# Tokens of the first two pairs by two queues, and two warming-up products fewer

## The chip, the cores and the metric

The kernel runs on one core of a Trainium2 chip. A core has a matrix engine (TensorE, PE in the profile; its weight loads are PEld), a vector engine (VectorE, DVE), a scalar engine (ScalarE, ACT), GpSimd (POOL) and a sync engine (SyncE, SP). Transfers between the chip's main memory and the on-chip memory run on 16 DMA engines; here SP and ACT issue them, each into a queue of its own (q1 is SP's, q10 is ACT's in the trace). The metric is the time of one execution on the device in microseconds; lower is better.

## The reference

The input is 16 sequences (B) of 256 tokens (T) of 128 features (C). Twelve layers of attention without softmax follow each other, each with 16 heads of 8 features; then a layer norm of input plus result, a feed-forward block and a second layer norm:

```
x = inputs
for i in range(12):
    q, k, v = split(x @ Wqkv[i].T + bqkv[i])       # heads of 8 features
    att = einsum('bhqd,bhkd->bhqk', q, k) / sqrt(8)
    y = einsum('bhqk,bhkd->bhqd', att, v)
    x = y @ Wproj[i].T + bproj[i] + x
x = layernorm(inputs + x)
g, u = x @ (w_gate/127).T, x @ (w_up/127).T
out = layernorm(x + (silu(g) * u) @ (w_down/127).T)
```

Since there is no softmax, the tokens enter the twelve layers only through their Gram matrix and their mean.

## The kernel before

The 16 sequences are taken as 8 **pairs** (PB = 2 batches each, L32 to L36), and the pairs as two **sets** of four (G = 4). Each pair has 512 tokens, 256 KB. Its tokens are loaded into `xtoks[p]`, a view of the tile `qgv` with four chunks of 128 tokens, each with a column of ones beside it (L220 to L223). Chunks 0 and 1 are the pair's first batch, 2 and 3 its second.

**Start.** VectorE fills `zero` and the columns of ones, and PE makes WARM = 30 products of zeros, which are used nowhere, while the first tokens are on their way (L224, L225). ACT issues the q weights of layer 0 (`wq0s`, L241), warms up its table (L243) and issues the biases (`bcol`, L244).

**Loads.** `load` (L263) hands the planner one operation on SP with a cost of 4 ns a KB. The loop at L268 asks for the tokens of the eight pairs, with prio -9 + 0.01 p. `prep_weights` (L279) asks for each layer's weights; layer 0's have prio -9 too (L282, L283).

**Prologue of a pair** (L326 to L355). `gram` makes four fp32 products on PE (L336, two records each in the trace), one for each chunk of 128 tokens, summed by batch. VectorE takes means from the sums (L340 to L342), PE turns them into rows (L346), ACT or VectorE copies these out (L349, a helper at L205 or L207), and VectorE takes the means' product off the Gram matrix (L353). Then come `products` (L455, the Gram matrix by the value weights), `heads` (L380 and L499, then L509 to L511 on VectorE and GpSimd, then L517), and `projection` (L529 and L530, L534 to L536, L541). From layer 1 on, products L434 to L444 come ahead of them. The q side of layer 0 is a copy of `wq0s` into each pair's `qgv` tile (`first_q`, L469), which must wait until the pair's Gram products have read the tokens there. At the end the feed-forward block goes pair by pair (L706 to L736).

**Who sets the order.** Every operation from the loads on goes through `Plan`. It holds a cost for each engine that could do the operation, and the operations that must come before it. `run` (L118) repeats one step: it finds the earliest start of each operation whose predecessors are placed, and among those that could start first it takes the one with the lowest number

```
(_, end, e), o = min(((b, o) for b, o in found if b[0] <= first), key=lambda x: (x[1].prio - TAILW * x[1].tail, -x[1].tail, x[1].n))
```

with TAILW = 0.0001 (L53, L145). The tail of an operation is its own least cost, plus 300, plus the longest tail of the operations that use its result:

```
o.tail = min(o.costs.values()) + 300 + max((u.tail for u in o.users), default=0)
```

(L124). The engines then carry out their instructions in the order in which the planner placed them, and real waits are semaphores on the data. The planner believes that a load is there 3000 ns after its end on SP (AFTER, at the head of the planner's part). Instructions that are issued outside the planner, such as L241 and L244 on ACT, come ahead in their engine's order; the planner doesn't know of them.

Of the kernel before, what the change touches and what calls it, by code (L numbers as in the profile page):

```python
# [21 lines left out]
C = 128  # L22
# [3 lines left out]
PB = 2  # L26
NP = B // PB
# [7 lines left out]
N = PB * T  # L35
K = N // 128  # L36
G = 4
NO = NP // G
OB = G * PB
WARM = 30  # L40


OSTEP = 0.5
# [148 lines left out]
def linear_attention_ffn_kernel(ctx: ExitStack, tc: tile.TileContext, x, xt, wall, wq0, bias, wg, wu, wd, out):  # L192
    nc = tc.nc
# [27 lines left out]
    xtoks = [t.rearrange("p (k c) -> p k c", c=C + 1) for t in qgvs]  # L221
    for t in xtoks:
        nc.vector.memset(t[:, :, C:], 1.0)  # L223
    for _ in range(WARM):  # L224
        nc.tensor.matmul(banks[7][:, :128], zero, zero, start=True, stop=True)  # L225
# [11 lines left out]
    mhalf = new("mhalf", [K])  # L237
    nc.gpsimd.memset(mhalf, -0.5)

    bcol, wq0s = new("bcol", [L, 4]), new("wq0s", [C])  # L240
    nc.scalar.dma_start(wq0s, wq0)  # L241

# [20 lines left out]
    def load(dst, src, vs, prio, kb=256, reads=[]):  # L263
        plan.op({SP: kb * 4}, lambda e: nc.sync.dma_start(dst, src), reads, vs, prio)


    vq, vgv = [Val() for _ in range(NP)], [Val() for _ in range(NP)]
    for p in range(NP):  # L268
        load(xtoks[p][:, :, 0:C], x[p * N : (p + 1) * N, :].rearrange("(k p) c -> p k c", p=128), [vq[p], vgv[p]], -9 + 0.01 * p)

# [528 lines left out]
```

## Time and profile before

| What | us |
|---|---|
| median of four runs (lowest, highest) | 305.72 (305.21, 306.1) |
| the execution that was profiled | 306.1 |
| its span, first to last instruction | 304.1 |
| PE busy | 294.9 (97%) |
| VectorE busy | 226.6 (75%) |
| ACT busy | 218.0 (72%) |
| GpSimd busy | 138.0 (45%) |
| first warming-up product on PE | 1.04 |
| first Gram product on PE | 4.28 |
| SP's issue of tokens and first weights | 0.79 to 6.29 |
| ACT's issue of q weights, of biases | 0.79, 5.04 |

How to read it: all times within the profile count from the span's first instruction. "Busy" of an engine is the union of its instructions' times. A line such as L336 is a line of the kernel file; where a helper issues an operation, the line is the helper's. The chain of waits is followed back from the last instruction, at each step to what released it. A queue's rows give its packets, megabytes and the share of 16 engines' time. Of a DMA, the profile gives when it was issued and the time from there to its landing.

### The profile page before, as it was taken

To read this page: it belongs to the slowest core of one execution; us is meant where nothing else is said; L and a number is where in the kernel's file an instruction comes from. 1 tells how busy PE (TensorE), PEld (TensorE's weight loads), DVE (VectorE), ACT (ScalarE), POOL (GpSimd) and SP (SyncE) were. 2 spreads that over 40 slices of the span, in tenths; PEclk is the share of its full clock that TensorE was granted. 3 is DMA by queue.
4 is the path that set the end of the run, shared out by engine and by line. 5 is a ranking of instruction groups with operands and counts; after the bars stand their busy time and mean duration, and the time that the engine had idled before them with its cause. 6 is when DMAs were issued, how large, how long until landed. Compare 5 with 4: busy or idle time off the path is not lost.

```text
span 304.1 us, 12834 instructions
## 1 busy us (share of the span) xinstructions
PE 294.9 (97%) x5376; PEld 270.3 (89%) x5376; DVE 226.6 (75%) x683; ACT 218.0 (72%) x559; POOL 138.0 (45%) x208
## 2 busy tenths in 40 slices
PE   8999999999999999999999999999999999999981
PEld 8989999999999999999998999989999998878760
DVE  4796877777677676876767777776654789999993
ACT  3557777767777768777686676776787658778875
POOL 8146452334531445215431354234431157777883
PEclk9999999999999999999999999999999999999999
DMA  7634213112031130311302101220000000000225
GB/s 213 159 95 125 72 39 86 40 42 85 3 88 37 40 88 4 88 41 28 98 2 56 37 11 47 57 63 22 2 2 2 5 1 2 0 0 6 66 70 138
DMA packets 22489, 15.65 MB, mean 51 GB/s; under 512 B 1952, under 2 KB 19872, under 8 KB 22432
## 3 DMA queue, kind: packets, MB, share of 16 engines
q1 hardware_dynamic: 21872, 14.62, 17.7%
q8 instruction: 42, 0.69, 0.9%
q10 hardware_dynamic: 560, 0.22, 0.3%
q14 instruction: 15, 0.12, 0.1%
HBM read 8.02 MB, written 2.10 MB: 33 GB/s over the span
## 4 chain that ended last, share of the span: by engine, by line
PE 87%; DVE 10%; issue 1%; ACT 1%; POOLq 0%; POOL 0%; DVEq 0%
PE bank L455 14%; PE bank L434 8%; PE bank L517 8%; PE bank L436 7%; PE bank L435 7%; PE bank L442 5%; PE bank L499 5%; PE bank L536 4%; PE bank L534 4%; PE bank L535 4%; PE bank L443 3%; PE bank L444 3%; PE bank L336 3%; DVE st L618 2%; PE bank L706 2%; PE bank L707 2%
## 5 line engine op out<-in xcount | busy, mean ns | idle before, releaser
L210 POOL TENSOR_TENSOR thl<-tst,thl 128x260 fp32r<-128x260 f32 x88 | 64.9, 768 | 123.6 <-ACT thl L205 123.6
L205 ACT COPY qgv<-bank 128x256 f32<-128x256 f32 x169 | 59.9, 378 | 19.0 <-PE bank L444 12.8
L205 ACT COPY kv<-bank 128x512 f32<-128x512 f32 (+1 forms) x93 | 53.4, 576 | 19.8 <-PE bank L436 14.4
L434 PE MATMUL bank<-whl,thl 128*128 128x256 f32 x176 | 51.9, 295 | 0.0
L436 PE MATMUL bank<-whl,thl 128*128 128x256 f32 x176 | 49.7, 282 | 0.0
L435 PE MATMUL bank<-whl,thl 128*128 128x256 f32 x176 | 49.4, 281 | 0.0
L455 PE MATMUL bank<-kv,g 128*128 128x128 f32 x352 | 46.1, 275 | 0.0
L541 DVE TENSOR_TENSOR tst<-bank,tst 128x260 f32<-128x260 f32 x96 | 36.9, 424 | 9.7 <-PE bank L536 9.3
L205 ACT CAST thl<-tst 128x260 fp32r<-128x260 f32 x88 | 33.0, 408 | 14.5 <-DVE tst L541 14.4
L455 PEld LDWEIGHTS bank<-kv,g 128*128 128x128 f32 x352 | 42.7, 191 | 0.4 <-issue 0.4
L448 DVE TENSOR_SCALAR qgv<-bank,bcol 128x2 f32<-128x2 f32 x88 | 19.1, 220 | 28.3 <-ACT qgv L205 22.9
L434 PEld LDWEIGHTS bank<-whl,thl 128*128 128x128 f32 x176 | 33.1, 188 | 4.0 <-issue 3.8
L530 DVE TENSOR_TENSOR yhl<-bank,yhl 128x260 fp32r<-128x260 f32 x96 | 34.4, 418 | 2.2 <-ACT yhl L205 2.1
L436 PEld LDWEIGHTS bank<-whl,thl 128*128 128x128 f32 x176 | 33.1, 188 | 0.2 <-POOL thl L210 0.2
L435 PEld LDWEIGHTS bank<-whl,thl 128*128 128x128 f32 x176 | 33.2, 189 | 0.0
L442 PE MATMUL bank<-thl,whl 128*128 128x260 f32 x88 | 28.8, 327 | 0.0
L205 ACT CAST yhl<-bank 128x260 fp32r<-128x260 f32 (+1 forms) x61 | 22.0, 408 | 8.5 <-PE bank L517 7.9
L207 DVE CAST yhl<-bank 128x260 fp32r<-128x260 f32 (+1 forms) x43 | 16.8, 430 | 13.0 <-PE bank L517 13.0
L517 PE MATMUL bank<-qgv,gm 32*32 32x130 f32 x1536 | 26.1, 280 | 0.4 <-issue 0.2
L443 PE MATMUL bank<-thl,whl 128*128 128x260 f32 x88 | 24.8, 282 | 0.0
L444 PE MATMUL bank<-thl,whl 128*128 128x260 f32 x88 | 24.7, 281 | 0.0
L517 PEld LDWEIGHTS bank<-qgv,gm 32*32 32x32 f32 x1536 | 17.3, 103 | 5.9 <-issue 0.5
(157 smaller groups left out, 696.0 us busy)
## 6 DMA issues: line engine op xcount, KB each, us to landing
wraw<-wall SPq DMA_DIRECT2D x12, 256.0 KB, 2.9
wpt<-whl SPq DMA_DIRECT2D x24, 96.0 KB, 2.2
qgv<-x SPq DMA_DIRECT2D x8, 256.0 KB, 5.0
xt<-xt SPq DMA_DIRECT2D x8, 256.0 KB, 3.2
out<-kv SPq DMA_DIRECT2D x7, 256.0 KB, 2.3
wpt<-whl SPq DMA_DIRECT2D x24, 64.0 KB, 2.7
wpt<-whl SPq DMA_DIRECT2D x24, 32.0 KB, 1.9
wraw<-wg SPq DMA_DIRECT2D x1, 192.0 KB, 3.5
```

The lines of the kernel that those rows point to most:

```text
L205: nc.scalar.copy(dst, src)
L210: (nc.vector if e == DVE else nc.gpsimd).tensor_tensor(dst, a, b, ALU.subtract)
L434: nc.tensor.matmul(o, hi[:, b, 0:C], hl(0, 1, 2), start=True, stop=False)
L435: nc.tensor.matmul(o, hi[:, b, 0:C], hl(1, 1, 2), start=False, stop=False)
L436: nc.tensor.matmul(o, lo[:, b, 0:C], hl(0, 1, 2), start=False, stop=True)
L442: nc.tensor.matmul(o, hl(0, 0), flat(hi), start=True, stop=False)
L443: nc.tensor.matmul(o, hl(0, 0), flat(lo), start=False, stop=False)
L444: nc.tensor.matmul(o, hl(1, 0), flat(hi), start=False, stop=True)
L455: nc.tensor.matmul(bank(pgv)[:, b * C : (b + 1) * C], g0[p][:, b, :], tv(b), start=True, stop=True)
L517: nc.tensor.matmul(bank(pys[r])[group(g + r), b * W : (b + 1) * W], gm[group(g), r * PB + b, :], qss[p][group(g), b, :], start=True, stop= ...
L530: plan.op({DVE: dve(PB * W)}, lambda e: nc.vector.tensor_tensor(yl, bank(py)[:, : PB * W], yh.bitcast(F32), ALU.subtract), [py, vyh[p]], [ ...
L541: plan.op({DVE: dve(PB * W)}, lambda e: nc.vector.tensor_tensor(ts, bank(pw)[:, : PB * W], ts, ALU.add), [pw], [vt[p], vc[p]], prio)
```

## The change

The number of warming-up products goes from 30 to 28. The tokens of pairs 0 and 1 (SPLIT = 2) are loaded in two halves: ACT issues the second batch of each, ahead of the q weights and the biases and outside the planner; SP loads the first batch through the planner, with a cost for 128 KB in place of 256 KB. The other six pairs are loaded as before.

```diff
-WARM = 30
+SPLIT = 2
+WARM = 28
...
     nc.gpsimd.memset(mhalf, -0.5)
 
+    half = lambda a, b: a[:, b * (K // PB) : (b + 1) * (K // PB)]
+    tokens = [x[p * N : (p + 1) * N, :].rearrange("(k p) c -> p k c", p=128) for p in range(NP)]
+    for p in range(SPLIT):
+        nc.scalar.dma_start(half(xtoks[p], 1)[:, :, 0:C], half(tokens[p], 1))
+
     bcol, wq0s = new("bcol", [L, 4]), new("wq0s", [C])
     nc.scalar.dma_start(wq0s, wq0)
...
     vq, vgv = [Val() for _ in range(NP)], [Val() for _ in range(NP)]
     for p in range(NP):
-        load(xtoks[p][:, :, 0:C], x[p * N : (p + 1) * N, :].rearrange("(k p) c -> p k c", p=128), [vq[p], vgv[p]], -9 + 0.01 * p)
+        cut = (lambda a: half(a, 0)) if p < SPLIT else (lambda a: a)
+        load(cut(xtoks[p])[:, :, 0:C], cut(tokens[p]), [vq[p], vgv[p]], -9 + 0.01 * p, 256 // (1 + (p < SPLIT)))
```

## The prediction

> **What bounds the kernel now.** I read the page first: TensorE (PE) is busy for nearly the whole span, so what delays PE at the start delays everything behind it.
>
> ```profile
> PE 294.9 (97%) x5376; PEld 270.3 (89%) x5376; DVE 226.6 (75%) x683; ACT 218.0 (72%) x559; POOL 138.0 (45%) x208
> ```
>
> The stretches of the span say the same: PE is busy 60.00 of 60 us from 60 to 120, 59.82 from 120 to 180, 59.83 from 180 to 240 and 39.61 of 40 from 240 to 280. So I take a delay of the first products one to one to the end. The chain of waits from 0.7 to 9 us (start, us, what) is PE alone:
>
> ```profile
> 1.04 3.38 PE bank L225 x30
> 4.42 2.56 PE bank L336 x16
> 6.98 0.22 PE bank L346 x2
> 7.20 0.90 PE bank L336 x8
> 8.10 0.22 PE bank L346 x2
> ```
>
> Thirty warming-up products, then the gram products (L336): eight records a pair, two pairs, then one pair at a time. Eight take 0.90 later, so sixteen should take 1.8; these take 2.56. Two reasons. The weight loads show a small wait for tokens (a gap of 0.10 between the last warming-up load and the first gram load):
>
> ```profile
> 4.00 0.15 PEld L225 LDWEIGHTS <-zero 128*128 128x128 bf16 x1
> 4.25 0.29 PEld L336 LDWEIGHTS bank<-qgv 128*128 128x128 f32 x1
> ```
>
> And up to 5.70 PE goes at half speed: gram products start 0.214 us apart before that point and 0.112 after it (starts of single instructions; the granted-clock column says 1.00 throughout and doesn't show this). In two stretches of 1.40 us each, the gram products and their loads:
>
> ```profile
> 4.30:5.70 1.40, 1.40 (x6) 1.40 (x7) 1.00 1.07 265
> 5.70:7.10 1.40, 1.34 (x12) 1.26 (x12) 1.00 1.01 322
> ```
>
> So a microsecond gained or lost before 5.70 is worth half a microsecond, one after it a whole one.
>
> Next the queues. SP issues four pairs, layer 0's weights, four pairs; ACT issues the q weights at 0.79 and the biases at 5.04:
>
> ```profile
> 0.79 2.08 SPq L264 DMA_DIRECT2D qgv<-x  x4
> 2.92 0.50 SPq L283 DMA_DIRECT2D wraw<-wall  x1
> 3.46 2.83 SPq L264 DMA_DIRECT2D qgv<-x  x4
> ```
>
> The DMA answers for the first four issues, one by one (issue times 0.79, 1.28, 1.82, 2.37; last figure: us from issue to landing):
>
> ```profile
> qgv<-x SPq DMA_DIRECT2D x1, 256.0 KB, 3.4
> qgv<-x SPq DMA_DIRECT2D x1, 256.0 KB, 3.7
> qgv<-x SPq DMA_DIRECT2D x1, 256.0 KB, 4.4
> qgv<-x SPq DMA_DIRECT2D x1, 256.0 KB, 4.8
> ```
>
> They land at 4.2, 5.0, 6.2 and 7.2, about 1.0 us for each 256 KB. PE loads the first pair at 4.25, the second at 5.82, the third at 6.93 and the fourth at 8.04 (single starts): slack 0.8, 0.7 and 0.8, none on the first.
>
> **What the change does to the order.** The diff halves the planner cost of pairs 0 and 1 (from 256 x 4 = 1024 to 512). The planner (L145) takes, of loads that could start at once, the one with the lowest prio - 0.0001 x tail, and the tail holds the load's own cost (L124). Pairs 0 to 3 have the same operations behind them, so the same tail; only prio, -9 + 0.01 p, orders them now. With 512 less tail, pairs 0 and 1 go back by 0.0001 x 512 = 0.0512, which is more than the 0.02 between pair 0 and pair 2. Against a common number: pair 2 at 0.02, pair 3 at 0.03, pair 0 at 0.0512, pair 1 at 0.0612. So **SP issues pair 2, pair 3, then the halves of 0 and 1**, and PE, which the planner puts in order by the same arrival times, starts with gram products of pairs 2 and 3. The weights, now behind the fourth load, lie further back and stay there. The halves that ACT sends at 0.79 belong to pairs wanted third and fourth. (Planner costs are used here for order only, never as times.)
>
> **Part by part.** *Two warming-up products less* (30 start in 1.04 to 4.11, 0.107 apart): PE is free 0.21 earlier, at about 4.0. It waits for tokens in any case: 0. If the tokens were there, 0.21 at half speed would be worth 0.11.
>
> *Pair 2 first, 256 KB by SP, with ACT's 256 KB beside it where 64 KB of q weights lie now.* Packets by queue (q1 is SP, q10 is ACT) from 2.75 to 3.25, then from 3.25 to 3.75:
>
> ```profile
> q1 hardware_dynamic: 248, 0.13, 84.3%
> q10 hardware_dynamic: 91, 0.04, 27.9%
> ...
> q1 hardware_dynamic: 341, 0.17, 112.1%
> ```
>
> 339 packets with two queues, 341 with one: from 2.75 on the queues share one rate. Before that ACT's came on top (SP 91 alone in 1.75 to 2.25; 111 and 48 in 2.25 to 2.75). SP's first pair is 512 packets: 91 + 111 + 248 = 450 by 3.25, the rest 0.09 later. If ACT goes on, SP has between half of 340 per 0.5 us (372 by 3.25, the rest 0.41 later: 0.32 late) and the 73% seen (0.03 late). I take 0.2 late: landing 4.4, first load about 4.45. Ends: 0.2 early (64 KB no longer beside it, at the 332 to 338 GB/s of these rows) and 0.6 late (equal shares throughout: 512 KB are down now at 5.0, less those 64 KB). At half speed 0.2 is worth **+0.1**, the ends -0.1 and +0.3.
>
> The Trainium skill (DMA: Bandwidth & Descriptors, "Issuing engines are not separate DMA queues") speaks against the change: a transfer started on another engine runs on the same 16 DMA engines and saves only issue time. The rows agree from 2.75 us on and disagree before it. By the rule alone pair 2 would share from its first packet, and the sum would be some 0.1 us higher.
>
> *Pair 3 second.* It is whole when SP has moved 512 KB; ACT's 320 KB (two halves, q weights) go beside it, 832 KB in all. Today 832 KB are down when the third pair lands: 3 x 256 + 64, at 6.2. The second gram would be due at 5.82 + 0.1, and a load comes some 0.1 after the landing: 6.3 instead of 5.92, a wait of about 0.35, at full speed; I take **+0.3**, as most of that landing's 16 parts come earlier than its last. Ends: 0 (ACT gives way; 512 KB are down at 5.0) and 0.4.
>
> *Pairs 0 and 1 third and fourth.* At 960 and 1088 KB, so 6.2 to 7.2, and due from 7.3 and 8.4: 0, hidden behind grams of pairs 2 and 3. Weights and pairs 4 to 7 have the same bytes before them as now: 0.
>
> *ACT's queue.* q weights land behind two halves, near 6; their copies (5.55, 6.58, 7.69 on ACT) are first read by L517 at 18.66. Biases go out at 5.04 now, just when the second pair lands, though ACT was done with its warming-up at 3.20; with two more DMAs ahead I expect 5.7 to 6.3. Behind that issue stand the first copies; ACT idles 2.36, 0.61 and 0.71 us before the first three, which covers it. The biases are first read at 15.33. Cost 0; without that cover, the row copies at 8.35 would come late and cost what exceeds 0.3. SP still issues nine DMAs and then idles from 6.3 to 9.49, which hides a later issue: 0.
>
> *The planner behind it.* Weights come one pair's cost earlier in its list, so it may put a gram ahead of an L455, or layer 1's weight cast on ACT. PE's sum of work is the same: 0, but with ends of 0.6 either way, one late or early cast (0.42) and subtraction (0.35) in the stage at 19.67 to 20.78, where the chain runs over VectorE.
>
> **Sum:** 0 + 0.1 + 0.3 = +0.4. The profiled execution took 306.1 (span 304.1, 2.0 around it), so 306.5 by its own terms; it is the slowest of four, whose median is 305.72. On that: **306.1**, +0.13%; the ends of the terms but the planner's (-0.1 to +0.7) make 305.6 to 306.4. About 0.2% (0.61 us) is what a measurement of this kernel can tell from no change.
>
> **Rivals.** *It does what it says*: pair 0 comes first, in halves. For it: the diff's plain text. Against: the 0.0512. SP's half of pair 0 then needs 256 packets instead of 512, landing about 0.5 earlier; PE starts at 4.0 instead of 4.25 at half speed: -0.12, and -0.1 more at most: 305.5.
>
> *The clock opens late (the other side).* Full speed came 4.66 us after the first product (1.04 to 5.70). A hole of 0.1 didn't hinder it; I expect one of 0.3 to 0.5 at 4.0 to 4.5. If a hole of that length makes the count start anew, it opens near 4.45 + 4.66 = 9.1: 3.4 us more at half speed cost 1.7, 307.8. It decides from whatever hole length counts as idle, which no row here shows. Against it: a hole this short is a tenth of the stretch.
>
> *The planner's new order hits a tight stage.* Slower: +0.6 on top, 306.7. Faster: -0.7 on the median if a stage loosens, 305.0 (the middle is full, so only the first 25 us and the last 15 offer anything).
>
> **Chances.** Forecast 0.56, of which 0.10 over 306.33 (both ends late: 0.7); does what it says 0.06 (0.01 of it faster); late clock 0.08; new order slower 0.20, faster 0.10. So faster 0.11, same 0.51, slower 0.38. The range leaves out the late clock and about a tenth more: 305.1 to 306.9.
>
> **What would show it.** Right: the first SP load is waited for by the first gram, with PE idle 0.3 to 0.5 after the 28th warming-up product; SP's row has two issues of 256 KB ahead of two of 128; sixteen gram products end near 7.2 instead of 6.98 with a wait inside; from there the stretches look as before, 0.4 later. Wrong: a first gram at 4.0; 128 KB issues first on SP; half-speed products after 6; or an equal start and a different last 15 us, which would be the planner's order.

## The result

Times in us. "Before" was timed again beside the changed kernel.

| | median | lowest to highest | executions |
|---|---|---|---|
| before | 305.78 | 304.83 to 306.66 | 76 |
| changed | 305.89 | 305.39 to 308.28 | 53 |
| changed, those up to 306.5 | 305.73 (mean 305.79) | 305.39 to 306.5 | 38 |
| changed, those from 307.06 on | mean 307.69 | 307.06 to 308.28 | 15 |

The ratio is 1.0019, 95% interval 1.001 to 1.0028: a loss of 0.6 us in the mean (306.33 against 305.74). The median, 0.11 higher, hides how it comes about. The changed kernel's times form two groups with nothing between 306.5 and 307.06, and before has no execution over 306.66 in these 76. The lower group's mean is 0.05 above before's; nearly all of the loss is the 15 executions of the upper group (15/53 x 1.9 = 0.54).

The execution that was profiled is one of the lower group: 305.59, span 303.9. So its profile shows what the change costs when all goes well, and not the loss.

### The profile page after: what moved, and what is told of

Read it like the earlier page. It is cut to its first block, busy times and chain, and to the rows that moved or that the text cites. A ratio compares the mean times of both kernels' runs of the same rounds, so it can differ in the third digit from the quotient of the medians.

```text
span 303.9 us, 12833 instructions
## 1 busy us (share of the span) xinstructions
PE 294.6 (97%) x5374; PEld 270.0 (89%) x5374; DVE 229.2 (75%) x686; ACT 217.2 (71%) x559; POOL 136.5 (45%) x205
## 4 chain that ended last, share of the span: by engine, by line
PE 86%; DVE 10%; DMA 1%; issue 1%; ACT 1%; POOLq 0%; POOL 0%; DVEq 0%
PE bank L462 14%; PE bank L441 8%; PE bank L524 8%; PE bank L443 7%; PE bank L442 7%; PE bank L449 5%; PE bank L506 5%; PE bank L543 4%; PE bank L541 4%; PE bank L542 4%; PE bank L450 3%; PE bank L451 3%; PE bank L343 3%; DVE st L625 2%; PE bank L713 2%; PE bank L714 2%
## 5 line engine op out<-in xcount | busy, mean ns | idle before, releaser
L206 ACT COPY kv<-bank 128x512 f32<-128x512 f32 (+1 forms) x90 | 51.6, 575 | 19.3 <-PE bank L443 13.5
L524 PE MATMUL bank<-qgv,gm 32*32 32x130 f32 x1536 | 25.9, 280 | 0.2 <-DVE gm L214 0.2
L524 PEld LDWEIGHTS bank<-qgv,gm 32*32 32x32 f32 x1536 | 17.4, 103 | 5.3 <-ACT kv L206 0.4
```

The lines of the kernel that those rows point to most:

```text
L206: nc.scalar.copy(dst, src)
L524: nc.tensor.matmul(bank(pys[r])[group(g + r), b * W : (b + 1) * W], gm[group(g), r * PB + b, :], qss[p][group(g), b, :], start=True, stop= ...
```

## The profile after

The busy times are close to those of before:

```profile
PE 294.6 (97%) x5374; PEld 270.0 (89%) x5374; DVE 229.2 (75%) x686; ACT 217.2 (71%) x559; POOL 136.5 (45%) x205
```

PE's timeline from 0 to 8 us (start, busy, line, operation, number of products; in brackets the idle time ahead and what ended it):

```profile
1.04 3.17 PE L226 MATMUL bank<-zero 128*128 128x128 bf16 x28 [1.04 <-DVE qgv L224]
4.62 2.58 PE L343 MATMUL bank<-qgv 128*128 128x129 f32 x16 [0.41 <-DMA qgv<-x]
7.03 0.38 PE L353 MATMUL bank<-ident,means 128*128 128x128 f32 x2
7.25 1.06 PE L343 MATMUL bank<-qgv 128*128 128x129 f32 x8
```

The 28 warming-up products are over at 4.21, and PE then has nothing to do for 0.41, until the first tokens have landed. No second wait follows: the other 15 gram products and the next pair's come without a bracket. In two stretches cut where the trace records full clock, at 5.78 (before: 5.70), the gram line alone (columns: PE busy with its products, PEld busy with its loads, granted clock, DMA share, GB/s) has 5 products in 1.18 us and 13 in 1.22:

```profile
4.60:5.78 1.18, 1.17 (x5) 1.18 (x6) 1.00 1.22 290
5.78:7.00 1.22, 1.22 (x13) 1.22 (x11) 1.00 1.10 334
```

The granted-clock column says 1.00 in both. The change of pace shows only in the counts.

Which tokens land when, from the DMA answers (size, then us from issue to landing), issue by issue. First SP's, issued at 0.79, 1.29 and 1.82:

```profile
qgv<-x SPq DMA_DIRECT2D x1, 256.0 KB, 3.7
qgv<-x SPq DMA_DIRECT2D x1, 256.0 KB, 4.5
qgv<-x SPq DMA_DIRECT2D x1, 128.0 KB, 4.5
```

Whole pairs come first on SP, and the half of pair 0 third. The first whole pair lands at 4.48 (the chain of waits has 3.69 from 0.79), the second at 5.8, pair 0's half at 6.3. ACT's two halves, both issued by 1.3, land at 4.2 and 5.9. ACT's own timeline:

```profile
0.79 1.05 ACTq L244 DMA_DIRECT2D qgv<-x  x2
1.87 0.52 ACTq L247 DMA_DIRECT2D wq0s<-wq  x1
...
6.29 0.40 ACTq L250 DMA_DIRECT2D bcol<-bias  x1
6.87 0.71 ACT L206 COPY qgv<-wq0s 128x256 f32<-128x256 f32 x2 [2.95 <-PE bank L343]
```

**Where the time went in this execution.** I laid the starts of the 24 groups of 64 small products (L517 before, L524 after) of the two traces side by side. The first comes 0.20 later than before, the second 0.30, and those from the third to the sixteenth, at 162 us, 0.31. Inside the sixteenth, before loses 0.53 that the changed kernel doesn't, and from there on the changed kernel is 0.21 to 0.23 ahead, which is the span's 0.2. That loss at 162 comes and goes by execution (last section); it isn't the change's.

## The experiments

Two theories stood against each other for the upper group. **Late clock**: the hole between the warming-up products and the first gram is sometimes long enough that full clock comes one step later. **Planner's order**: the order of pairs 2, 3, 0, 1 meets a tight stage in some executions. Beside them the sizes of the prediction's terms were to be tested. The median of before stands beside each group of runs, since it differs by chip.

**The order undone, the halves kept** (before 305.82). Only the cost argument goes, so that the planner takes the pairs 0 to 3 in order again:

```diff
-        load(cut(xtoks[p])[:, :, 0:C], cut(tokens[p]), [vq[p], vgv[p]], -9 + 0.01 * p, 256 // (1 + (p < SPLIT)))
+        load(cut(xtoks[p])[:, :, 0:C], cut(tokens[p]), [vq[p], vgv[p]], -9 + 0.01 * p)
```

> The changed kernel with the full planner cost (1024) for all eight loads, so that SP issues the halves of pairs 0 and 1 first and PE keeps the order of before. Theory (the planner's new order makes the hole in front of the first Gram products, and the hole makes the clock open late in about a quarter of the executions): first SP half lands by 3.9, first Gram load at 3.9 to 4.05, no hole over 0.15, no group of times above 307, and a median 0.1 to 0.3 under before (305.78). Rival (two queues at the start are the harm, whatever the order): first Gram load after 4.3, group above 307 stays, median 305.9.

Measured: 306.07 (305.24 to 306.98, 12 executions), ratio 1.0007 (0.9988 to 1.0027), none over 307. SP's first half lands at 3.34, ACT's at 3.59, and the first gram starts at 4.00, with no hole. So the cost argument alone makes the order, and with the pairs in order the upper group isn't seen in 12. The gain of an early start isn't there, though, and PE's timeline shows who takes it:

```profile
4.00 2.15 PE L343 MATMUL bank<-qgv 128*128 128x129 f32 x16
...
6.55 1.16 PE L343 MATMUL bank<-qgv 128*128 128x129 f32 x8 [0.17 <-DMA qgv<-x]
```

The clock opened at 4.31 in this execution, the grams of two pairs were done at 6.2, and the third waited for pair 2, which landed at 6.51. Here the third landing bounds the start, not the first.

**The hole filled** (same chip): the changed kernel with 34 warming-up products.

```diff
-WARM = 28
+WARM = 34
```

> The changed kernel with 34 warming-up products in place of 28, so that PE has no hole while it waits for pair 2; all else as in the changed kernel. Theory (the hole makes the clock open late): no executions above 306.8, the rest as in the changed kernel within 0.1 to 0.2, so a mean of 305.8 to 305.9 and a ratio to before near 1.000. Rival (the late group comes from elsewhere, late landings or a reordered stage): 15 of 53 above 307 as in the changed kernel, ratio near 1.002.

Measured: 305.77 (305.1 to 306.45, 12), ratio 0.9998 (0.9981 to 1.0014). The first pair landed as late as in the changed kernel (4.49), and the first gram starts at 4.64 with no idle time ahead of it:

```profile
4.64 2.71 PE L343 MATMUL bank<-qgv 128*128 128x129 f32 x16
```

The upper group is gone with the hole, and the order is unchanged: this speaks for the late clock.

**A hole in the kernel before** (same chip): 24 warming-up products in place of 30.

```diff
-WARM = 30
+WARM = 24
```

> The kernel before with 24 warming-up products in place of 30; loads, queues and order as before. It makes a hole of some 0.45 (by PE's records) in front of the first Gram products, with no other part of the change. Theory (the hole alone opens the clock late): two groups of times, some 15 to 50 in 100 executions 1.5 to 2.5 above the rest, ratio 1.002 to 1.004. Rival (the hole is harmless, the landings or the order are not): one group, 304.8 to 306.7, ratio 0.999 to 1.001.

Measured: 305.62 (304.95 to 306.79, 12), ratio 0.9998 (0.9977 to 1.0019). A hole of 0.44 is there, the median is before's, and no upper group is set apart:

```profile
4.22 2.26 PE L336 MATMUL bank<-qgv 128*128 128x129 f32 x16 [0.44 <-DMA qgv<-x]
```

So "any hole makes the clock late" fell, and the theory had to say how long the hole must be.

**The order alone**, on two chips (before 305.82 and 305.34): the kernel before with the changed costs, and nothing loaded by ACT.

```diff
-        load(xtoks[p][:, :, 0:C], x[p * N : (p + 1) * N, :].rearrange("(k p) c -> p k c", p=128), [vq[p], vgv[p]], -9 + 0.01 * p)
+        load(xtoks[p][:, :, 0:C], x[p * N : (p + 1) * N, :].rearrange("(k p) c -> p k c", p=128), [vq[p], vgv[p]], -9 + 0.01 * p, 256 // (1 + (p < 2)))
```

> The kernel before with only the planner's cost of pairs 0 and 1 halved: whole pairs by SP in the order 2, 3, 0, 1, all 30 warming-up products, no tokens by ACT. Theory (the order does harm only because ACT's halves share the rate): first Gram load at 4.25 as before, no group above 307, ratio 0.998 to 1.001; the planner's new order downstream shows alone, and the 0.5 that PE loses at 162 us in the trace of before and not in the changed one may go. Rival (the new order costs by itself): ratio above 1.001.

> Once more the kernel before with only the planner's cost of pairs 0 and 1 halved (whole pairs by SP in the order 2, 3, 0, 1; 30 products), for a narrower interval. Theory (the order by itself costs nothing, and takes layer 1's weights to SP's queue at 6.3 in place of 14.3): no late group, median 0.0 to 0.3 under before, ratio 0.998 to 1.000. Rival (the earlier 0.9988 was chance): ratio 1.000 to 1.0015.

Measured: 305.68 (304.86 to 306.33, 12), ratio 0.9988 (0.9971 to 1.0005), and 305.09 (304.5 to 306.34, 12), ratio 0.9992 (0.9977 to 1.0008). None of the 24 is in an upper group, so the order theory fell: no cost of the new order is seen, and the intervals leave room for 0.0008 of the time at most. Both medians are a little under before's (0.14 and 0.25), but neither interval leaves 1 out.

**The changed kernel again** (before 305.89), unedited, for a profile of a late execution.

> The changed kernel itself once more, beside the next three. Theory (its hole of 0.4, longer in some executions when pair 2 lands late, makes the clock open a window later): 2 to 6 of 12 executions between 307.0 and 308.3, none of them with a clock that opened before 8, the rest 305.3 to 306.5. Rival (the late group of the first 53 came from one chip or one session): none above 307, median 305.7 to 305.9.

Measured: 306.0 (305.44 to 307.99, 12), ratio 1.0014 (0.9999 to 1.0029). Two of the twelve are late (307.95, 307.99), and the profiled one is the last of these. Its first pair landed at 4.70. PE's timeline, and the gram line in three stretches (columns as above):

```profile
4.83 3.78 PE L343 MATMUL bank<-qgv 128*128 128x129 f32 x16 [0.62 <-DMA qgv<-x]
8.40 0.64 PE L353 MATMUL bank<-ident,means 128*128 128x128 f32 x2
```

```profile
4.90:6.60 1.70, 1.70 (x8) 1.70 (x9) 1.00 1.19 311
6.70:8.60 1.90, 1.90 (x9) 1.61 (x8) 1.00 1.17 319
8.80:10.20 1.40, 1.37 (x7) 1.40 (x8) 1.00 1.21 292
```

The hole is 0.62 and not 0.41, and half speed lasts until 10.2: eight products in 1.70 us, nine in 1.90, seven in 1.40, always some 0.21 each, where the other execution took 0.1 each from 5.78 on. The sixteen grams take 3.78 in place of 2.58. The trace records full clock from 10.205 on for 293.55 us; in the 305.59 execution from 5.78 on for 296.96. The two lengths differ by 3.41, but a length alone doesn't tell a late opening: in the second profile of the order alone it is 293.55 as well, with an opening at 6.02. The groups of small products, up to the sixteenth, start 2.4 to 2.6 later than before's. This is the prediction's late-clock rival, seen.

**Longer holes in both kernels**: fewer warming-up products in the kernel before (18 beside 305.89, 21 beside 305.34) and in the changed one (22 beside 305.89).

```diff
-WARM = 30
+WARM = 18
```

```diff
-WARM = 28
+WARM = 22
```

```diff
-WARM = 30
+WARM = 21
```

> The kernel before with 18 warming-up products in place of 30: a hole of about 1.1 in front of the first Gram products, with loads, queues and order as before. 24 products made a hole of 0.44 and no late group. Theory (the length of the hole decides): a late group of a quarter to two thirds of the executions, 1.5 to 2.0 above the rest, mean 306.3 to 307.0. Rival (not the hole, but how ACT's halves and the new order spread the arrivals): one group up to 306.9, mean 305.6 to 306.0.

> The changed kernel with 22 warming-up products in place of 28, so that its hole grows from 0.4 to about 1.05. Theory (length of the hole): the late group grows from 28% to over half of the executions, mean above 306.7. Rival (the hole is not it): 28% or none, mean as the changed kernel's, 305.9 to 306.4.

> The kernel before with 21 warming-up products in place of 30: a hole of about 0.7, between the 0.44 of 24 products (none of 12 late) and the 0.8 to 1.1 of 18 (8 of 8 at or above 306.4). Theory (the length of the hole decides, somewhere between 0.41, which passed, and 0.62, which failed): part of the executions late, a quarter to all of those whose window holds the hole, mean 306.1 to 306.8. Rival (no threshold of length): as with 24 products, mean 305.7 to 305.9 and none over 307.

Measured: 306.79 (306.42 to 307.95, 8), ratio 1.0039 (1.0022 to 1.0056); 307.05 (306.4 to 308.07, 6), ratio 1.0046 (1.0029 to 1.0064); and 307.14 (305.17 to 307.55, 12), ratio 1.0053 (1.0036 to 1.007). Full clock comes at 8.50, 9.26 and 9.97. The first gram line of each, in that order:

```profile
3.96 3.78 PE L336 MATMUL bank<-qgv 128*128 128x129 f32 x16 [0.81 <-DMA qgv<-x]
```

```profile
4.71 3.78 PE L343 MATMUL bank<-qgv 128*128 128x129 f32 x16 [1.14 <-DMA qgv<-x]
```

```profile
4.06 3.78 PE L336 MATMUL bank<-qgv 128*128 128x129 f32 x16 [0.60 <-DMA qgv<-x]
```

The 3.78 is the mark of sixteen grams wholly at half speed. The kernel before, in its own order and with its own loads, becomes late when its hole is made long: with 21 warming-up products one execution stands at 305.17 and the other 11 at 306.29 and more, with 18 all 8 at 306.42 and more. The hole makes the upper group, in either kernel.

**The kernel before with 28** (before 305.89): what the two warming-up products are worth by themselves.

```diff
-WARM = 30
+WARM = 28
```

> The kernel before with 28 warming-up products, the one part of the change that touches no load. Theory 1 (28 alone costs and gains nothing at the start, since the first pair lands at 4.14 anyway): first Gram load 4.25, no late group, ratio 0.999 to 1.001. Theory 2 (the 0.5 that PE loses inside L517 near 162 us in the trace of before hangs on where its instruction stream is cut, which two products fewer shift): the loss is gone from the trace and the median 0.3 to 0.6 lower, ratio 0.998 to 0.999. If the loss stays, the planner's order removed it in the changed kernel.

Measured: 306.2 (305.27 to 307.41, 12), ratio 1.001 (0.9993 to 1.0028); no clear cost. Of the 0.53 that before's profile loses near 162 us, 0.08 is left here, but the median isn't lower, so the second theory isn't borne out. The first pair landed at 3.76 in the profiled execution, ahead of the last warming-up product, so there is no hole; the clock opened at 6.65, on time. That execution (306.74) lost 0.92 elsewhere. From the timelines of VectorE and PE:

```profile
20.36 0.73 DVE L207 CAST whl<-wraw 128x512 fp32r<-128x512 f32 x1 [0.82 <-DMA wraw<-wall]
```

```profile
22.16 0.39 PE L536 MATMUL bank<-yhl,whl 128*128 128x260 f32 x1 [1.12 <-DVE yhl L530]
```

Layer 2's weights landed late, VectorE waited for them with its cast, and the casts that PE waited for stood behind it. This is the tight stage that the prediction feared; in this execution a late landing hits it, with the pairs in their old order. This kernel's 307.24 and 307.41 may be of that kind. So may the few executions of before over 307 in these runs (307.45, 307.57); none of those was profiled.

**ACT's halves later** (before 305.34): the changed kernel with its two halves issued behind the q weights and the biases.

```diff
-    for p in range(SPLIT):
-        nc.scalar.dma_start(half(xtoks[p], 1)[:, :, 0:C], half(tokens[p], 1))
-
     bcol, wq0s = new("bcol", [L, 4]), new("wq0s", [C])
     nc.scalar.dma_start(wq0s, wq0)
...
+    for p in range(SPLIT):
+        nc.scalar.dma_start(half(xtoks[p], 1)[:, :, 0:C], half(tokens[p], 1))
```

> The changed kernel with ACT's two halves issued behind the q weights, the table's warming-up and the biases (about 3.3 or later) in place of first; the planner's order 2, 3, 0, 1 and 28 products stay. Theory (ACT's halves take rate from pairs 2 and 3, which are wanted first): pair 2 lands at 3.8 to 4.4 in place of 4.5 to 4.7, pair 3 near 5.0 to 5.3 in place of 5.8, no late group, mean 305.6 to 305.9. Rival (the landing moved for another reason, as SP's order or the chip's state): pair 2 still after 4.45, late group as in the changed kernel.

Measured: 311.55 (310.57 to 312.21, 5), ratio 1.0203 (1.018 to 1.0226). Half of the expectation held: with no halves beside them the first two pairs landed at 4.36 and 5.26, and the hole was 0.28 with full clock from 4.41. The time went the other way. From ACT's timeline, the waits of PE, and three stretches (busy time of PE, PEld, DVE, ACT and POOL, then the granted clock):

```profile
5.69 0.35 ACTq L247 DMA_DIRECT2D bcol<-bias  x1
6.17 1.08 ACTq L249 DMA_DIRECT2D qgv<-x  x2
```

```profile
PE bank L342 <- DMA qgv<-x: 4.3, 2, 4.0
```

```profile
7.00:11.00 4.00, 0.20 (x2) 0.00 (x1) 0.85 (x4) 1.02 (x3) 0.49 (x5) 1.00 1.17 312
12.00:14.60 2.60, 2.60 (x14) 2.60 (x14) 1.15 (x7) 0.78 (x2) 0.66 (x3) 0.50 0.00 0
14.60:16.00 1.40, 1.40 (x14) 1.40 (x13) 1.19 (x6) 0.58 (x2) 0.23 (x2) 0.98 0.37 94
```

The bias issue waited until 5.69, the halves went out behind it at 6.17 and landed 5.0 after that; PE stood for 4.0 and then had half its clock for 3.41. So in this program a transfer can't be put back on the second queue by a little; the last section says what its issue waited for.

**Order alone, with the q weights late** (before 305.34): nothing at all beside SP's first pair.

```diff
-    nc.scalar.dma_start(wq0s, wq0)
     nc.scalar.activation(new("warm", [1]), mhalf[:, 0:1], AF.Silu)
+    nc.scalar.dma_start(wq0s, wq0)
     nc.scalar.dma_start(bcol, bias)
```

> The order-only kernel (see above) with the q weights issued by ACT behind the table's warming-up, about 3.2, so that nothing lies beside SP's first pair. Candidate for a version that beats both. Theory (what lies beside the first pair sets its landing): first landing 0.1 to 0.3 earlier than with q weights first (3.76 to 4.40 seen), ratio 0.997 to 0.9995. Rival (the first landing is bound by SP's own packets, 450 of 512 by 3.25): landing 3.8 to 4.4 as now, ratio 0.999 to 1.001.

Measured: 310.12 (309.26 to 310.23, 4), ratio 1.0155 (1.0133 to 1.0177). The first pair landed at 3.55, the earliest of all runs. But the q weights were issued at 5.72 only, landed 6.0 later, and ACT's first copy waited 8.61 for them:

```profile
11.80 1.02 ACT L205 COPY qgv<-wq0s 128x256 f32<-128x256 f32 x3 [8.61 <-DMA qgv<-x]
```

Behind it PE ran dry, and its clock was halved from 14.49 to 17.91.

## Why the prediction was right, and where it was wrong

**The time and the range.** 306.1 was forecast with a range of 305.1 to 306.9; the median is 305.89. That the mean loss of 0.6 lies so near the forecast 0.4 is luck. The 0.4 was to be paid by every execution; those without the late clock lie 0.05 above before in the mean, and the other 0.54 come from a rival that the forecast held apart. In the one profile of the lower group the start is 0.2 to 0.3 late in place of 0.4; the times of the group show 0.05 of it.

**The planner's order: right.** SP's row and PE's grams come in the order 2, 3, 0, 1, worked out from 512 x 0.0001 against 0.02. Undoing the cost alone brings the old order back.

**PE bound, half price ahead of the clock: right.** The first gram load comes 0.33 later (4.58 against 4.25), the second pair's first product 0.21 later (6.14 against 5.93): of the 0.33, 0.16 is lost by the half price, and the clock's 0.08 later opening adds 0.04.

**Two products less: 0 by itself, which the run with 28 doesn't contradict** (ratio 1.001, 0.9993 to 1.0028). But they are part of the hole: the 0.21 that they leave is half of the 0.41, and with six more (34) the hole and the upper group are gone. The prediction costed them at nothing because PE waits for tokens anyway; the waiting itself had a price.

**Pair 2's landing: mechanism right, size low.** Forecast 0.2 late, measured 0.34 (4.48 against 4.14). Over the profiles the first 256 KB land at 3.76 to 4.40 with only the q weights beside them (eight profiles, mean 4.09) and at 4.48 to 4.70 with ACT's halves beside a whole pair (four profiles, mean 4.56): about 0.5 late, near the end that the prediction gave for equal shares. On the rule that a second queue saves only issue time (the Trainium skill, DMA: Bandwidth & Descriptors, "Issuing engines are not separate DMA queues"): these landings lie nearer to it than to the 73% that I took from the rows. In the changed kernel SP had 162 of 298 packets from 2.75 to 3.25 and 232 of 361 in the next half microsecond, 54% and 64%. The count of packets doesn't time a landing by itself, though: by it the first pair of before was whole at 3.34, and it landed at 4.14. By the trace's packet records its last packet ended at 3.65, in the changed kernel at 3.77, and the landing came 0.49 and 0.71 behind. So 0.12 of the 0.34 lies in the packets.

**Pair 3's wait: wrong.** Forecast a landing at 6.2 and +0.3; it landed at 5.8 and PE didn't wait. This was the largest term of the sum, and it was 0. The step that failed is the reading that 832 KB are down when before's third pair lands. Up to 5.0, before and then changed (queue, packets, MB, share of the 16 engines):

```profile
q1 hardware_dynamic: 1532, 0.77, 57.3%
q10 hardware_dynamic: 144, 0.07, 4.5%
```

```profile
q1 hardware_dynamic: 1116, 0.56, 39.4%
q10 hardware_dynamic: 539, 0.26, 19.5%
```

In before the 832 KB (0.85 MB) were down near 5.0, and the third pair landed at 6.26. In the changed kernel SP's first two pairs (0.52 MB) were down by about 5.0 with 0.26 MB of ACT's beside them, and landed at 5.8. A landing trails its last packet, by 0.95 for the one and 0.76 for the other. The prediction counted that time as time for bytes, and put all 320 KB of ACT's ahead. The two queues together weren't faster than SP's with the q weights beside it (0.82 against 0.84 MB). What sets the time from the last packet to the landing, no run shows.

**ACT's queue: right.** Biases at 6.29, forecast 5.7 to 6.3; no wait of PE for the first copies, at 6.87, is seen. SP, though, issues a tenth DMA and not nine: layer 1's weights leave at 6.87 (14.29 before). No cost or gain of it is seen.

**Downstream: right at 0 in this pair of traces** (0.31 from the second group to the sixteenth). The start's 0.20 became 0.30 between the first and second group, in the stage at 20 us; I have no cause for that 0.10.

**The clock rival: the mistake that mattered.** The price was near (1.7 forecast; the groups lie 307.69 - 305.79 = 1.9 apart). The mechanism was right in that a hole delays full clock, not in that a count starts anew with the first gram: that would put full clock 4.66 after it, and it comes 4.5 to 5.9 after it in the four late profiles. One step of 3.41 fits them better (worked out below). What failed most is the form: "a chance of 0.08" took it for a yes or no for the kernel. It is a share of executions (hole and clock both vary from one profile to the next), and a share of 15 in 53 at 1.9 is the whole loss. The prediction also measured the hole against "a tenth of the stretch" and stopped there, when its own landing range (to 4.8) made holes up to 0.7 possible.

The length goes with the late group in these runs. The holes are counted from the modelled end of the last warming-up product; from where the next one would have started they are about 0.2 longer.

| hole, us (profiled execution) | kernel | its executions |
|---|---|---|
| none; 0.11 in one profile of the order alone | order undone; 34 products; order alone, twice | none of 48 over 306.98 |
| 0.41 and 0.62 | changed, both samples | 17 of 65 at 307.06 or more, none between 306.5 and there |
| 0.44 | before, 24 products | none of 12 over 306.79, median 305.62 |
| 0.60 | before, 21 | 11 of 12 at 306.29 or more, median 307.14 (before there: 305.34) |
| 0.81 | before, 18 | all 8 at 306.42 or more, median 306.79 |
| 1.14 | changed, 22 | all 6 at 306.4 or more, median 307.05 |

The changed kernel's first pair landed at 4.48 and 4.70, which puts its hole at 0.41 (clock on time) and 0.62 (late); this fits the mixture.

The Trainium skill (TensorE: Matmul & The Clock Gate, "Part 1: The HAM clock gate") says that the array's clock is halved until one window of 4096 cycles, 3.41 us, has been busy, and that the windows run free of the kernel's start. The traces agree: in the traces of before and of the 305.59 execution full clock lasted 296.96 us (87 x 3.413), in the late one 293.55 (86 x 3.413), and without a long hole it began anywhere between 3.85 and 6.65. In the four late profiles it began at 8.50 to 10.21, and one window earlier is 5.09 to 6.79; the whole hole lies in the window that ends there. In the 305.59 execution the window from 2.37 to 5.78 holds the whole hole of 0.41, and the clock opened. This also gives part of the spread of both kernels: up to 2.8 us of half speed more or less, worth half of that.

**Not settled.** The limit lies between 0.41 and 0.60 by the profiles if length alone counts, and the times of the run with 24 products speak for more than 0.44; where in a window the hole lies may count too. In the run with 24 products the clock opened at 3.85, when the hole had hardly begun, so that profile says nothing of its hole, and only its twelve times do. It does say something against length alone: its window, from 0.43, starts 0.61 before PE's first product at 1.04, and the clock opened all the same, where a hole of 0.60 in the run with 21 held it back. As for the twelve times, a few of them (306.45 to 306.79) can't be told from the upper end of kernels without a hole. Of the changed kernel's 17 late executions one was profiled; that the others had long holes is inferred. No kernel here is clearly faster than both: the order alone, at 0.9988 and 0.9992, comes nearest.

## What to carry to other kernels

Where an edit changes a planner's cost, work out the order that follows first: a smaller load became a later one, and the second queue's halves raced the pair that was now first. While the clock is still to open, keep the matrix engine without a gap up to the latest landing, not the usual one: warming-up products cost nothing here while tokens are awaited (34 against 28), and gaps of 0.6 us and more cost 0.9 to 1.9 us. Compare the spread of many executions before you read a profile: two groups mean that one profile shows only one of them.

## What the runs showed of the hardware

**An issue waits for a landing, by a semaphore that the program uses again.** In the kernel before, the biases leave at 5.04 as SP's second load has landed (5.02); in the changed kernel SP's next four leave from 4.25 on, as ACT's first half has landed (4.24), and the biases at 6.29, behind the landing of pair 0's half (6.27). SP had been idle from 3.35, and ACT from 3.20 and 3.91. The records of the issues in the traces say why: the loads use eight semaphores in turn, and each of these issues waits for the one that it is to use again, so the wait belongs to the program as it was built. It is not a wait for data that the issue needs, and the planner doesn't know of it. With the halves or the q weights behind such an issue they left at 6.17 and 5.72, 0.02 after the landings at 6.15 and 5.70, and landed 5 to 6 us later, and the kernels took 311.55 and 310.12. No run with more semaphores was made.

**A clock that is open closes again.** After 4.0 us of idle PE, half speed came back at 11.23 for 3.41 us, and in the last run from 14.49 to 17.91. There the granted-clock column does show it (0.50), and in the first microseconds it doesn't.

**Small products lose time near 162 us in some executions.** The profile before, then the one after, of the sixteenth group of 64:

```profile
161.75 0.99 PE L517 MATMUL bank<-qgv,gm 32*32 32x130 f32 x55
162.92 0.43 PE L517 MATMUL bank<-qgv,gm 32*32 32x130 f32 x9 [0.18 <-issue]
```

```profile
162.05 1.07 PE L524 MATMUL bank<-qgv,gm 32*32 32x130 f32 x64
```

In the traces a 16 KB transfer of instructions (queue q8) starts a little before. Where it starts 1.05 us ahead of the group, 0.53 is lost (before); at 1.19, 0.36 (24 products); at 1.34, 0.22 to 0.25 (the late execution); from 1.63 on, at most 0.08 (eleven profiles). A loss of 0.5 in one profile is as large as the effects that were studied here, and it would have passed for a gain of the change. That the transfer causes it is a guess from these pairs.
